# The second half of the first batch normalized on GpSimd and projected inside the first score steps, and the last projection moved ahead in the MLP

## The chip, the cores and the metric

The kernel runs on one core of a Trainium2 chip. The metric is the device time of one execution in microseconds (us). Five engines work side by side: TensorE (PE; its weight loads are shown apart as PEld), VectorE (DVE), ScalarE (ACT), GpSimd (POOL) and SyncE (SP), which issues DMAs. Each engine takes its instructions in program order and waits at semaphores for the others. TensorE writes into PSUM banks of 128 partitions x 512 float32; VectorE and ScalarE read them out.

## The reference

A block of attention and a gated MLP, with four layer norms, on x of shape (4, 1024, 256). The weights of the attention are binarized (sign times the mean magnitude of a row), those of the MLP are ternary.

```python
def attn(x, Wq, bq, Wk, bk, Wv, bv, Wp, bp):      # 16 heads of 16
    q, k, v = (split_heads(binlinear(x, W, b)) for W, b in ((Wq, bq), (Wk, bk), (Wv, bv)))
    att = softmax(einsum('bhtd,bhsd->bhts', q, k) * 16 ** -0.5)
    y = einsum('bhts,bhsd->bhtd', att, v)
    return binlinear(merge_heads(y), Wp, bp)

def ffn(x, ...):                                   # 256 -> 1024 -> 1024 -> 1024 -> 256
    h = silu(tlin(x, w1_w, w1_s)) * tlin(x, w2_w, w2_s)
    h = gelu(tlin(h, h1_w, h1_s))
    h = gelu(tlin(h, h2_w, h2_s))
    return tlin(h, w3_w, w3_s)

x = x + layernorm(attn(layernorm(x), ...))
x = x + layernorm(ffn(layernorm(x), ...))
```

## The kernel before

**Precision.** Activations that enter a product with signs or ternary weights are kept as two pieces, a rounded high part (`fp32r`) and the rest, so each product is made twice, once for each piece.

**Opening.** The tokens of the first batch come in two halves of 512. Ahead of the attention function, the first half is measured, normalized (L264), transposed (L284) and split into its two pieces (L286, L287). The second half is only measured (`measure_half(1)`). In the attention function's opening (from L1009), `norm(1, nc.vector)` normalizes the second half (L465), `first_heads(is_q, 0)` (L561) makes the queries and keys of the first four heads for the first half of the tokens: four products of 512 columns (L566), two reads of the bank by ScalarE (L572 with the scale and bias into the high part, L579 into `full`), and one VectorE instruction (L584 for queries, L587 for keys). `turn(1, k)` (L474) then transposes the second half in four products for each of two halves of the channels (L477), ScalarE copies the result (L482) and VectorE makes the rest (L485).

**Steps.** Attention is one software pipeline over steps (L1073 on); a step covers four heads. `first = -10`; a step s makes the first pass of tile s + 10 (scores of 128 queries x 512 keys for four heads, L722, each head in 32 rows of the array; VectorE takes their maxima, L731), and from s = 0 the second pass (scores again with the maximum subtracted, L768, exponentials by ScalarE, L778) and the product with the values (L794). A tile's number a tells which halves it needs: tiles 0 to 3 take first-half queries with first-half keys, tiles 4 to 7 first-half queries with second-half keys, tiles from 8 on second-half queries. When eight tiles are done, `combine` joins the maxima and `shift` (L748) turns them for the second pass.

Within a step the four heads start at slots 0, 0, 1 and 3 of five (`BEGIN`), and `run_jobs` puts side jobs at two places of the step: slot 0 behind the third of the five, slot 1 behind the last. `place((s, slot), job)` files a job. TensorE meets, in a step, three score products left over from the tile before, the slot 0 jobs, five score products of the new tile, the slot 1 jobs. The side jobs of the opening are `first_heads(.., 1)`, `value(m)` (L494, eight products of 256 columns and a copy by ScalarE), the four `part` jobs of group 0 (L535, four products of 512 columns; at steps first + 2, + 4, + 6, + 8, slot 1, written by GpSimd in L548 and L549), `alphas`, `projection_bias` (L405). Jobs of one place run in the order in which they were filed.

**Banks.** `bank()` (L305) hands out the seven PSUM banks by a planned clock; `put` and `got` state the true waits, and `got` makes each reader of a bank wait for the readers before it.

**GpSimd in the opening.** The root for the second half (L166), fills of `negmax`, of the ones in the value tiles (L436, L437), of `yn` (L441) and of `bits` (L903), two products with the identity for the value bias (L397). It is idle from 19.8 us to the copies of `part` at 35.2 us.

**MLP.** Eight blocks of 512 tokens. `hidden` (L1256) makes eight columns of 128 hidden units: for the first three columns the products of all but the last two inputs are made first, then each column is finished, passed through Gelu by ScalarE and split by VectorE (L1188, L1189), and then the jobs filed for the column in `beside` run. `norm` measures and normalizes the next block's tokens, `turn` transposes them. In block 0, `scale_y` (L1394) scales the last batch's attention output and `last_projection` (L1399) projects it (L1407), scales and shifts it (L1412, L1413), normalizes it and adds it to x. The tiles with the tag "z" have two buffers, which `norm`, `last_projection` and `down` share in turn.

Of the kernel before, what the change touches and what calls it, by code (L numbers as in the profile page):

```python
# [34 lines left out]
AF = mybir.ActivationFunctionType  # L35
ALU = mybir.AluOpType
# [10 lines left out]
def sandwich_kernel(  # L47
# [24 lines left out]
    nc = tc.nc  # L72
    B, T, C = x.shape
    F = w1T.shape[1]
    KC = C // P
# [70 lines left out]
    alpha4 = small.tile([P, 2], F32, tag="alpha4", name="alpha4", bufs=1)  # L146
    bias4 = small.tile([P, 2], F32, tag="bias4", name="bias4", bufs=1)
# [142 lines left out]
    def attention(signs):  # L290


        with ExitStack() as actx:
# [6 lines left out]
            through = ps.tile([P, 7, 512], F32, tag="through", name="through")  # L300
# [29 lines left out]
            def got(banks, engine, access, for_pe=False):  # L330

                others = [o for o in ("PE", "ACT", "DVE") if o != engine and not (for_pe and o == "PE")]
                after = [i for b in banks for i in written[b] + read[b]]
                lasts = {"ACT": 500, "DVE": 580}[engine]
                clock[engine] = max(clock["PE"] + 240, clock[engine] + lasts)
                for b in banks:
                    read[b].append(access.ins)
                    free_at[b] = clock[engine] + lasts + 150  # L340
                return state(access, engine, after, others)
# [96 lines left out]


            yn = ac.tile([P, 16, 32], F32, tag="yn", name="yn")  # L440
            nc.gpsimd.memset(yn, 1.0)  # L441

            def half_tile(name, dtype=F32):

# [116 lines left out]
            def first_heads(is_q, j):  # L561

                t = bank()
                for k in range(KC):
                    for i in range(PIECES):
                        put(t, nc.tensor.matmul(  # L566
                            through[:, t, :], sign4["q" if is_q else "k"][:, k, :],
                            xnT_of[0][i][:, k, bass.ts(j, 512)],
                            start=(k == 0 and i == 0), stop=(k == KC - 1 and i == PIECES - 1),
                        ), xnT_by[0])  # L570
                to = (q_of[0][0] if is_q else k_of[0])[:, bass.ts(j, 512)]
                got([t], "ACT", nc.scalar.activation(  # L572
                    to, through[:, t, :], AF.Identity,
                    bias=bias4[:, 0:1] if is_q else k_bias4,
                    scale=alpha4[:, 0:1] if is_q else k_alpha4,
                ))
                full = a2.tile([P, 512], F32, tag="full", name=f"full4_{is_q}_{j}")
                n = 1 - is_q
                got([t], "ACT", nc.scalar.activation(  # L579
                    full, through[:, t, :], AF.Identity, bias=bias4[:, n : n + 1],  # L580
                    scale=alpha4[:, n : n + 1],
                ))
                if is_q:
                    nc.vector.tensor_sub(q_of[0][1][:, bass.ts(j, 512)], full, to.bitcast(F32))  # L584
                else:

                    nc.vector.scalar_tensor_tensor(  # L587
                        to, full, lower, to.bitcast(F32), ALU.mult, ALU.add
                    )
# [254 lines left out]
            def place(at, job):  # L844
                jobs.setdefault(at, []).append(job)

            first = -STEPS - LEAD
# [52 lines left out]

            raw_of = {}
            bits = ac.tile([P, 512], F32, tag="bits", name="bits")
            nc.gpsimd.memset(bits, 0)  # L903

            def weight_jobs():
                loads, stay, pass_by = [], [], []
# [83 lines left out]
            def alphas(n):  # L990

                t = bank()
                if n == "v":
                    for c in range(KC):
                        for k in range(KC):
                            put(t, nc.tensor.matmul(
                                through[:, t, c : c + 1], mag_of[n][:, k, bass.ts(c, P)],
                                avg[:, 0:1], start=(k == 0), stop=(k == KC - 1),
                            ))
                    got([t], "ACT", nc.scalar.copy(alpha_sb[:, 2, :], through[:, t, :KC]))  # L1000
                else:
                    for k in range(KC):
                        put(t, nc.tensor.matmul(
                            through[:, t, :C], avg, mag_of[n][:, k, :],
                            start=(k == 0), stop=(k == KC - 1),
                        ))
                    got([t], "ACT", nc.scalar.copy(az_bc, through[:, t, :C]))

            norm, turn, value = batch_jobs(0)  # L1009
            if signs:  # L1010
                quadrants(0)
                norm(1, nc.vector)
                for is_q in (True, False):
                    first_heads(is_q, 0)
                for k in range(KC):
                    turn(1, k)

                place((first, 1), lambda: first_heads(False, 1))
                place((first + 1, 1), lambda: first_heads(True, 1))
                for i, n in enumerate("vp"):  # L1020
                    place((first + 6 + i, 0), lambda n=n: alphas(n))
                after = first + 2
            else:
                part = group_jobs(0)
                norm(0, nc.vector)
                for k in range(KC):
                    turn(0, k)
                part(True, 0, nc.vector)
                norm(1, nc.vector)
                for k in range(KC):  # L1030
                    turn(1, k)
                part(False, 0, nc.vector)
                part(False, 1, nc.vector)
                part(True, 1)
                spread(0, (nc.sync, nc.scalar))
                after = first + 3
            for m in range(NT // 2):
                place((after + m, 0), lambda m=m: value(m))
            place((first + 8, 0), projection_bias)
            place((4, 0), load_scales)  # L1040

# [70 lines left out]
    def mlp(tag, low_too, wp):  # L1114
        with ExitStack() as fctx:
# [119 lines left out]
            def norm(blk):  # L1235
                mv, rs = stats([tokens(blk, i) for i in range(4)], f"f{tag}{blk}")
                xn_of[blk] = [pair_c(f"fxn{tag}_{blk}_{i}") for i in range(2)]
                for i in range(4):
                    nc.gpsimd.tensor_scalar(
                        xn_of[blk][i // 2][:, i % 2, :], tokens(blk, i), mv[:, i, 0:1],  # L1240
                        rs[:, i : i + 1], ALU.subtract, ALU.mult,
                    )
# [156 lines left out]
            def last_projection():  # L1399

                zs = [pair_c(f"z{tag}_{i}") for i in range(2)]
                zs = [zs[i // 2][:, i % 2, :] for i in range(4)]
                for m in range(2):
                    zp = ps_o.tile([P, 512], F32, tag="o", name=f"zp{tag}_{m}")
                    for i in range(2):
                        for k in range(KC):
                            nc.tensor.matmul(  # L1407
                                zp[:, bass.ts(i, C)], yT_last[:, k, bass.ts(2 * m + i, P)],
                                wp[:, k, :].bitcast(F32), start=(k == 0), stop=(k == KC - 1),
                            )  # L1410
                        z = zs[2 * m + i]
                        nc.vector.tensor_mul(z, zp[:, bass.ts(i, C)], az_bc)  # L1412
                        nc.vector.tensor_add(z, z, bz_bc)  # L1413
                mv, rs = stats(zs, f"z{tag}")
                for i, z in enumerate(zs):
                    nc.vector.tensor_scalar(
                        z, z, mv[:, i, 0:1], rs[:, i : i + 1], ALU.subtract, ALU.mult
                    )
                    to = x_sb[:, B - 1, NT // 2 + i, :]
                    nc.gpsimd.tensor_add(to, to, z)  # L1420
# [3 lines left out]
            for blk in range(blocks):  # L1424
                h = gated(blk)
                more = blk + 1 < blocks
                beside = {2: [lambda: norm(blk + 1)]} if more else {}
                beside2 = {3: [lambda: turn(blk + 1)]} if more else {}
                if blk == 0:
                    beside[6] = [scale_y]  # L1430
                    beside2[5] = [last_projection]
                if behind:
                    measure, finish = behind
                    beside[0] = [lambda: finish(*measure())]
                g1 = hidden(blk, "g1", h1_w, h1T, sh1_sb, h, beside)
                g2 = hidden(blk, "g2", h2_w, h2T, sh2_sb, g1, beside2)
                if more:
                    nc.scalar.activation(warm2, s3_bc[:, 0:1], AF.Silu)
                behind = down(blk, g2)
# [58 lines left out]
```

## Time and profile before

| what | value |
|---|---|
| median of three runs | 1567.8 us (1567.79 to 1568.9) |
| the profiled execution's own time | 1567.72 us |
| its span, first to last instruction | 1565.9 us |
| mean granted TensorE clock | 0.993 |
| last product ahead of the attention loop (L477) | ends at 22.5 us |
| first score product (L722) | 23.30 us |
| first second-pass product (L768) | 55.48 us |
| first product of the MLP (L1218) | 904.04 us |
| length of MLP block 0; of block 1 (first gate product to first gate product) | 87.4 us; 81.2 us |

The profile is of one execution. A busy TensorE is not TensorE at its peak, since the ends of matmuls are modelled; how far apart two products start says more. In the timeline a row is a start, a duration, an engine, a line, an operation with what it writes and reads, a count of merged instructions, and in brackets the idle time ahead of it and what ended it. The granted clock is the share of the full TensorE clock that the profile's records show.

### The profile page before, as it was taken

What the parts mean: (1) busy time and instruction counts of PE and PEld (TensorE: products, weight loads), DVE (VectorE), ACT (ScalarE), POOL (GpSimd) and SP (SyncE); (2) the same over time, 40 slices, a digit from 0 to 9 for tenths busy, and PEclk for the clock granted to TensorE, in tenths of its full rate; (3) what the DMA queues carried; (4) which work ended last, traced back from release to release, by engine and by line L of the source; (5) the groups of instructions that cost most, each with busy time, mean ns of one, the idle gap of its engine ahead of it and who ended that gap; (6) DMA issues with size and microseconds to landing.
All of it is one profiled execution on the core that took longest, in us unless ns stands there. A gap on an engine that the chain in (4) does not pass through costs nothing.

```text
span 1565.9 us, 31822 instructions
## 1 busy us (share of the span) xinstructions
PE 1531.1 (98%) x12988; PEld 980.3 (63%) x12988; DVE 1075.2 (69%) x1960; ACT 829.2 (53%) x1496; POOL 437.4 (28%) x595
## 2 busy tenths in 40 slices
PE   7999999999999999999999999999999999999998
PEld 5544445444444444454444477888888888888887
DVE  6889887899787798878899554554545544455453
ACT  4577777677777677777777841413232313232321
POOL 2223143564424563314612150120202020202010
PEclk8999999999999999999999999999999999999999
DMA  1311521133132033311312040000000000000000
GB/s 58 72 30 33 144 49 29 24 72 74 39 76 59 22 65 72 66 30 31 75 36 73 8 139 0 1 14 1 14 1 14 1 14 1 14 1 14 1 14 17
DMA packets 35084, 58.55 MB, mean 37 GB/s; under 512 B 9968, under 2 KB 21488, under 8 KB 34928
## 3 DMA queue, kind: packets, MB, share of 16 engines
q1 hardware_dynamic: 29760, 43.57, 12.8%
q0 software_dynamic: 3792, 11.54, 2.3%
q8 instruction: 104, 1.70, 0.4%
q10 hardware_dynamic: 1376, 1.31, 0.2%
q14 instruction: 52, 0.43, 0.1%
HBM read 24.40 MB, written 4.19 MB: 18 GB/s over the span
## 4 chain that ended last, share of the span: by engine, by line
PE 85%; DVE 9%; ACT 4%; issue 1%; POOL 1%; DMA 1%; SPq 0%; DVEq 0%; ACTq 0%; POOLq 0%
PE g L1218 30%; PE y L794 14%; PE through L768 12%; PE through L722 10%; PE p L1218 7%; DVE nm L731 5%; PE fzp L1332 4%; PE through L535 2%; ACT e L778 2%; PE through L494 1%; PE through L748 1%; PE through L637 1%; ACT ys L809 1%; DVE bnstp_x L175 1%; DVE yt L835 1%
## 5 line engine op out<-in xcount | busy, mean ns | idle before, releaser
L731 DVE TENSOR_REDUCE nm<-through 128x1 f32<-128x512 f32 x1024 | 643.5, 680 | 115.6 <-PE through L722 59.3
L778 ACT ACTIVATE e<-through 128x512 f32<-128x512 f32 x1024 | 545.4, 603 | 160.7 <-PE through L768 141.7
L722 PE MATMUL through<-ks,qs 32*128 32x512 f32 x2048 | 462.2, 445 | 3.8 <-DVE nm L731 2.7
L768 PE MATMUL through<-qs,ks 32*128 32x512 f32 x2048 | 442.6, 434 | 11.1 <-ACT e L778 7.3
L768 PE MATMUL through<-nmT,ones_r 32*128 32x512 f32 x1024 | 348.7, 450 | 0.4 <-ACT nmT L755 0.4
L794 PE MATMUL y<-e,v 128*32 128x256 f32 x4096 | 323.0, 393 | 0.0
L722 PEld LDWEIGHTS through<-ks,qs 32*128 32x128 f32 x2048 | 215.7, 184 | 106.4 <-issue 82.5
L1218 PE MATMUL g<-g,h_sb 128*128 128x512 f32 x1024 | 235.7, 390 | 0.0
L768 PEld LDWEIGHTS through<-qs,ks 32*128 32x128 f32 x2048 | 201.8, 183 | 44.6 <-ACT e L778 20.5
L1218 PEld LDWEIGHTS g<-g,h_sb 128*128 128x128 f32 x1024 | 191.7, 188 | 39.5
L768 PEld LDWEIGHTS through<-nmT,ones_r 32*128 32x128 f32 x1024 | 137.6, 182 | 91.7 <-issue 88.7
L794 PEld LDWEIGHTS y<-e,v 128*32 128x32 f32 x4096 | 86.5, 108 | 170.8 <-issue 150.7
L1261 ACT ACTIVATE g2f<-g,sh_sb 128x512 f32<-128x512 f32 x64 | 44.1, 688 | 200.5 <-PE g L1218 180.8
L1261 ACT ACTIVATE g1f<-g,sh_sb 128x512 f32<-128x512 f32 x64 | 44.1, 689 | 170.1 <-PE g L1218 166.9
L164 POOL TENSOR_SCALAR ve_fz<-mvp_fz 128x4 f32<-128x4 f32 (+1 forms) x8 | 1.9, 232 | 468.5 <-DVE mvp_fz L176 468.5
L1218 PE MATMUL g<-h,h1b_sb 128*128 128x512 f32 x512 | 126.4, 389 | 0.0
L1218 PE MATMUL g<-h,h1a_sb 128*128 128x512 f32 x512 | 126.4, 389 | 0.0
L1188 DVE CAST g<-g2f 128x512 fp32r<-128x512 f32 x64 | 27.8, 434 | 142.0 <-ACT g2f L1261 142.0
L1218 PE MATMUL p<-xnT_sb,w_sb 128*128 128x512 f32 x512 | 117.7, 390 | 0.0
L1218 PEld LDWEIGHTS g<-h,h1a_sb 128*128 128x128 f32 x512 | 96.1, 188 | 19.9
L1218 PEld LDWEIGHTS g<-h,h1b_sb 128*128 128x128 f32 x512 | 96.1, 188 | 19.9
L1218 PEld LDWEIGHTS p<-xnT_sb,w_sb 128*128 128x128 f32 x512 | 95.6, 188 | 19.9 <-issue 0.4
(204 smaller groups left out, 1515.8 us busy)
## 6 DMA issues: line engine op xcount, KB each, us to landing
qs<-h1b_sb SPq DMA_DIRECT2D x240, 64.0 KB, 2.4
ks<-h1b_sb SPq DMA_DIRECT2D x120, 64.0 KB, 2.4
wraw<-in_dram SPq DMA_DIRECT2D x28, 256.0 KB, 2.7
h_sb<-in_dram POOLq DMA_DIRECT2D x4, 1024.0 KB, 8.5
yT<-yt SPq DMA_DIRECT2D x112, 32.0 KB, 2.0
out_dram<-x_sb SPq DMA_DIRECT2D x7, 512.0 KB, 2.8
x_sb<-in_dram SPq DMA_DIRECT2D x3, 1024.0 KB, 5.3
w_sb<-in_dram POOLq DMA_DIRECT2D x3, 1024.0 KB, 8.4
```

The costliest lines, as they stand in the source:

```text
L175: nc.vector.bn_stats(st, z)
L494: put(t, nc.tensor.matmul(through[:, t, bass.ts(i, C)], xnT_of[b][j][:, k, bass.ts(2 * m + i, P)], w_in["v"][:, k, :], start=(k == 0 and j ...
L535: put(t, nc.tensor.matmul(through[:, t, :], w_in[tag][:, k, bass.ts(c, P)], xnT_of[b][i][:, k, bass.ts(j, 512)], start=(k == 0 and i == 0) ...
L722: put(t, nc.tensor.matmul(through[:, t, :], q_of[u][n][rows, bass.ts(qt, P)], k_of[u][rows, bass.ts(j, 512)], start=(n == 0), stop=(n == 1),))
L731: got([t], "DVE", nc.vector.tensor_reduce(nm_of[blk][:, n4, j, g : g + 1], through[:, t, :], AX.X, ALU.max, negate=True))
L768: t, nc.tensor.matmul(through[:, t, :], lhs, rhs, start=(n == 0), stop=(n == 2)),
L778: exps.append(got([t], "ACT", nc.scalar.activation(e_of[s, g], through[:, t, :], AF.Exp)))
L794: nc.tensor.matmul(y_of[blk][32 * g : 32 * g + 32, cols], v_sb[n // 2][:, n % 2, :, :].rearrange("p h d -> p (h d)")[:, bass.ds((4 * g4 + ...
L1188: nc.vector.tensor_copy(hi, full)
L1218: nc.tensor.matmul(out[c], wk, src[j][:, k, :], start=(k == 0 and i == 0 and j == 0), stop=(k == n_k - 1 and i == len(ws) - 1 and j == 1),)
L1261: nc.scalar.activation(g, ps, AF.Gelu, scale=scale[:, c : c + 1])
L1332: nc.tensor.matmul(out_ps[i][:, :C], g2[j][:, k, bass.ts(i, P)], wk, start=(k == 0 and n == 0 and j == 0), stop=(k == NF - 1 and n == len( ...
```

## The change

In the opening of attention, the second half's norm goes from VectorE to GpSimd, and its two transposes leave the place ahead of the first step: they become jobs of the steps `first + 1` (slot 1) and `first + 2` (slot 0). The second half's keys and queries for the first four heads move from the steps `first` and `first + 1` to both places of `first + 3`, the values from `first + 2` on to `first + 4` on, the alphas from `first + 6` and `first + 7` (slot 0) to `first + 5` and `first + 7` (slot 1). For the first half, the second read of the bank in `first_heads` goes from ScalarE to VectorE. The fills of `yn` and `bits` go to step `first + 4`. In the MLP's block 0, `scale_y` goes from column 6 to column 0 of the first hidden layer, `last_projection` from column 5 of the second hidden layer to column 2 of the first, and the next block's norm from column 2 to column 6 of the first; in `last_projection` the eight products of a bank now all stand ahead of VectorE's reads of it.

```diff
@@ -438,7 +438,6 @@
             yn = ac.tile([P, 16, 32], F32, tag="yn", name="yn")
-            nc.gpsimd.memset(yn, 1.0)
@@ -576,10 +575,16 @@
                 full = a2.tile([P, 512], F32, tag="full", name=f"full4_{is_q}_{j}")
                 n = 1 - is_q
-                got([t], "ACT", nc.scalar.activation(
-                    full, through[:, t, :], AF.Identity, bias=bias4[:, n : n + 1],
-                    scale=alpha4[:, n : n + 1],
-                ))
+                if j == 0:
+                    got([t], "DVE", nc.vector.tensor_scalar(
+                        full, through[:, t, :], alpha4[:, n : n + 1], bias4[:, n : n + 1],
+                        ALU.mult, ALU.add,
+                    ))
+                else:
+                    got([t], "ACT", nc.scalar.activation(
+                        full, through[:, t, :], AF.Identity, bias=bias4[:, n : n + 1],
+                        scale=alpha4[:, n : n + 1],
+                    ))
@@ -900,7 +905,6 @@
             bits = ac.tile([P, 512], F32, tag="bits", name="bits")
-            nc.gpsimd.memset(bits, 0)
@@ -1009,17 +1013,17 @@
                 quadrants(0)
-                norm(1, nc.vector)
+                norm(1, nc.gpsimd)
                 for is_q in (True, False):
                     first_heads(is_q, 0)
-                for k in range(KC):
-                    turn(1, k)
-
-                place((first, 1), lambda: first_heads(False, 1))
-                place((first + 1, 1), lambda: first_heads(True, 1))
+
+                place((first + 1, 1), lambda: turn(1, 0))
+                place((first + 2, 0), lambda: turn(1, 1))
+                place((first + 3, 0), lambda: first_heads(False, 1))
+                place((first + 3, 1), lambda: first_heads(True, 1))
                 for i, n in enumerate("vp"):
-                    place((first + 6 + i, 0), lambda n=n: alphas(n))
-                after = first + 2
+                    place((first + 5 + 2 * i, 1), lambda n=n: alphas(n))
+                after = first + 4
@@ -1038,6 +1042,8 @@
             place((4, 0), load_scales)
+            place((first + 4, 0), lambda: nc.gpsimd.memset(yn, 1.0))
+            place((first + 4, 0), lambda: nc.gpsimd.memset(bits, 0))
@@ -1408,6 +1414,7 @@
                                 wp[:, k, :].bitcast(F32), start=(k == 0), stop=(k == KC - 1),
                             )
+                    for i in range(2):
                         z = zs[2 * m + i]
                         nc.vector.tensor_mul(z, zp[:, bass.ts(i, C)], az_bc)
                         nc.vector.tensor_add(z, z, bz_bc)
@@ -1427,8 +1434,7 @@
                 beside = {2: [lambda: norm(blk + 1)]} if more else {}
                 beside2 = {3: [lambda: turn(blk + 1)]} if more else {}
                 if blk == 0:
-                    beside[6] = [scale_y]
-                    beside2[5] = [last_projection]
+                    beside = {0: [scale_y], 2: [last_projection], 6: beside[2]}
```

## The prediction

> **What bounds it now.** First the page: engines and chain.
>
> ```profile
> span 1565.9 us, 31822 instructions
> PE 1531.1 (98%) x12988; PEld 980.3 (63%) x12988; DVE 1075.2 (69%) x1960; ACT 829.2 (53%) x1496; POOL 437.4 (28%) x595
> PE 85%; DVE 9%; ACT 4%; issue 1%; POOL 1%; DMA 1%; SPq 0%; DVEq 0%; ACTq 0%; POOLq 0%
> ```
>
> TensorE carries 85% of the chain, so an edit is worth what it does to TensorE's idle time and rate. Second, TensorE alone in stretches of 3.41 us (columns: stretch, its length, busy us with instructions, granted clock, DMA), and then the timeline (start, us, engine, line, operation, count, wait ahead of it).
>
> ```profile
> 16.19:19.60 3.41, 2.58 (x6) 1.00 0.00 0
> 19.60:23.01 3.41, 2.88 (x11) 1.00 0.00 0
> 23.01:26.43 3.42, 2.67 (x18) 1.00 0.01 2
> 26.43:29.84 3.41, 2.57 (x10) 1.00 0.00 0
> 29.84:33.25 3.41, 3.41 (x14) 0.50 0.02 5
> 33.25:36.66 3.41, 3.41 (x12) 0.50 0.00 0
> 36.66:40.08 3.42, 3.42 (x19) 0.50 0.00 0
> 514.53:517.94 3.41, 2.56 (x28) 1.00 0.10 14
> 517.94:521.36 3.42, 3.42 (x32) 0.50 0.17 65
> ```
>
> ```profile
> 20.57 1.91 PE L477 MATMUL through<-ident,xn 128*128 128x128 f32 x8
> 23.30 0.73 PE L722 MATMUL through<-ks,qs 32*128 32x512 f32 x5 [0.82 <-DVE ks L587]
> ...
> 32.24 0.79 PE L535 MATMUL through<-xnT_sb,w_sb 128*128 128x512 f32 x1
> 32.83 0.63 PE L535 MATMUL through<-w_sb 128*128 128x512 f32 x1
> 33.26 0.63 PE L535 MATMUL through<-xnT_sb,w_sb 128*128 128x512 f32 x1
> 34.24 1.22 PE L722 MATMUL through<-ks,qs 32*128 32x512 f32 x3
> 35.39 0.58 PE L494 MATMUL through<-w_sb,xnT_sb 128*128 128x256 f32 x1
> ```
>
> The reader is to see that the clock changes only at multiples of 3.41 us, and that a busy TensorE does not decide it: 100% busy stretches stay at 0.50. I weighted each matmul's streaming time (half clock: 0.427 us per 512 columns, the step from 32.83 to 33.26; 0.213 for 256 columns or a 128-column float32 transpose) by the share of the array that it fills (a 32-row score product a quarter) and got for the seven opening stretches 0.72, 0.78, 0.49, 0.34, 0.76, 0.67, 0.82. Half clock ends after 0.78 and 0.82, not after 0.72, 0.76 or 0.67. Full clock is lost after 0.34; likewise after 0.36 at 514.53 us; the lowest share that kept it is 0.42. Up at about 0.77, down at about 0.4 fits every change in this trace. (The first clock record is at 23.01. Ahead of it the column shows 1.00, but L566's products start 0.43 us apart there and 0.23 from 24.49 on.)
>
> Third, the timeline of the MLP's first block, where the last projection sits, and one GpSimd row.
>
> ```profile
> 970.35 1.02 PE L1407 MATMUL zp<-wp_sb,yT_last 128*128 128x256 f32 x4
> 972.86 1.99 PE L1407 MATMUL zp<-wp_sb,yT_last 128*128 128x256 f32 x8 [1.49 <-DVE z L1412]
> 975.44 1.13 PE L1407 MATMUL zp<-wp_sb,yT_last 128*128 128x256 f32 x4 [0.59 <-DVE z L1412]
> ...
> 936.28 5.06 POOL L1239 TENSOR_SCALAR fxn<-x_sb,mvp_f,rsp_f 128x256 f32<-128x256 f32 x4
> ```
>
> TensorE stands still 1.49 + 0.59 us there, waiting for VectorE's reads of the same bank.
>
> **The change part by part.** *MLP.* With all products of a bank ahead of its reads, the 2.08 us go. But the projection now stands two columns after scale_y. TensorE gets there where it now begins column 3, at 929.56. Scale_y follows column 0's split on VectorE (until 929.9) and takes 0.88 for two rows: the second operand is there at 930.85, so 1.05 us of new wait, product time taken off. Net -1.0; ends -2.1 (no wait) and 0. Behind it VectorE holds the splits of columns 3 to 5 for about 9 us, until some 946, but the second hidden layer asks for them past 950: nothing. The norm moved to column 6 ends near 959 (2.1 statistics, 1.8 root, 5.06 GpSimd), its transposes come near 967: nothing; uncovered it would cost those 5 us.
>
> *Small moves.* Two GpSimd fills (1.04 us) go to step 4, where GpSimd idles between weight copies: nothing, 1.04 uncovered. The biased copy on VectorE (0.69 as L584; rows 0.43 to 0.78) still waits for ScalarE's read of its bank; keys are ready 0.1 us earlier (0 to 0.35), at 23.2. The moved steps issue no DMA; the first DMA copies of queries and keys slide on SP with their products.
>
> *Norm on GpSimd.* Four rows of 1.23 (up to 1.66 in this trace) from 18.85, behind the last fill: done at 23.8 to 25.5. TensorE asks at 24.65 (full) or 25.5 (half clock): nothing; worst 0.85.
>
> *Transposes and second-half projections, moved.* At 20.77 TensorE ends the first four-head products and waits for the keys until 23.2; the 1.91 us of transposes, which filled that hole, come two steps later. So the stretch that lifted the clock at 23.01 falls from 0.78 to 0.34 (1.17 us of products). The next ones hold score products and half-rate transposes: I count 0.64 and 0.50. From step 2 to 7 every step now carries two jobs, each 0.16 us of start-up gap and each followed by a score group that fills 1.15 us with 0.3 to 0.5 of array time: at best 0.74 in any stretch. The 0.82 that lifted the clock at 40.08 came from a step with one job, whose eight score products ran unbroken (37.40); the new order has such a step only at its start. So half clock until the second passes.
>
> Cost from 23.2 to the first second pass (55.48 now): 18 score groups, ten 512-column or value jobs, two transposes, the alphas, the projection bias, the shift. At half clock: 18 x 1.15 (34.24 to 35.39) + 10 x 2.0 (32.24 to 34.24) + 2 x 1.0 + 1.8 + 2 x 1.9 + 1.05 = 49.35, ending at 72.55: +17.1. At full clock (0.66 and 1.13, from 41.04 to 42.84 in the timeline; value 1.15, the rest 4.8 together) 28.1 plus 1.8 of waits for banks that VectorE holds, ending at 53.1: -2.4. Those are the ends; I take half clock, which the counted shares support. The clock then rises in the first second passes; one more stretch at half clock costs at most 1.7 (half of 3.41), I take 0.8 (0 to 5.1, three stretches).
>
> A rule speaks against this reading. The Trainium skill, "TensorE: Matmul & The Clock Gate", Part 4, says that transposes do not count as busy for the clock, and Part 1 that it falls after an idle window of about 3.4 us. Here it fell after a stretch with 0.84 us idle, and rose after one that was mostly transposes. By the page the transposes' absence costs no clock, and the sum would be the full-clock one below, 1564.3, not 1584.6.
>
> *Sum.* 1567.72 (this execution's own time, span 1565.9 plus 1.8 around it; the median of the runs is 1567.8) + 17.1 + 0.8 - 1.0 = 1584.6. Its own range: 1580 to 1589.
>
> **The rivals.** *A, clock back midway.* My best stretches are within 0.03 of the 0.77 that lifts it. Lifted at 43.5, in step 4: a half-done job and 3.5 us a step after it put the last first pass at 55.2 instead of 50.35: +4.85 - 1.0 = 1571.6; between 1568.5 and 1580 by the stretch.
>
> *B, faster: full clock throughout.* The early products run 17.0 to 20.8 without a hole, so in about half the positions of the 3.41 us grid one stretch passes 0.77 and lifts the clock near 20 to 21. If it then held, VectorE's maxima would run nearly unbroken from 24: -2.4 - 1.0, 1564.3. Against: the next stretch has under 0.8 us of array time, 0.24. It decides if the share that keeps full clock is in truth below that.
>
> *C, no gain, no loss.* Clock lifted near 33: the opening ends where it does now, and the -1.0 is below what can be told: 1567.
>
> **How the numbers follow.** 0.2% (3.1 us) is about what a measurement of this kernel can tell. Forecast 0.46, A 0.25, B 0.17, C 0.12. Of A four fifths lie above 1570.9: slower 0.46 + 0.20 = 0.66; B gives faster 0.17; C and the rest of A, same 0.17. The time is the forecast's, 1584.6. The range reaches down through A and C to 1565 and up to 1588, leaving out most of B and the forecast's top.
>
> **What would show it.** Granted clock 0.50 from the opening's first records to past 60 us; score groups 1.15 us apart from jobs of 2.0; the transposes in step 1 to 2 behind GpSimd's four rows; TensorE idle 20.8 to 23.2; L768 first at about 72; L1407 in one piece near 947 with one wait, for scale_y. Wrong: the clock column at 1.00 through 30 to 45 us, L768 before 55.5, or a GpSimd norm past 26 on which a transpose waits.

## The result, and the profile after

The changed kernel takes 1584.05 us (median of four runs, 1582.94 to 1585.72), the kernel before 1567.8 beside it (four runs, 1563.4 to 1568.9). The ratio is 1.0125, 95% interval 1.0102 to 1.0148: it is slower. The profiled execution took 1584.12 us, span 1582.3.

The page of the changed kernel, engines and chain:

```profile
span 1582.3 us, 31820 instructions
PE 1547.3 (98%) x12988; PEld 990.9 (63%) x12988; DVE 1073.3 (68%) x1958; ACT 828.0 (52%) x1494; POOL 442.6 (28%) x599
PE 85%; DVE 9%; ACT 3%; issue 1%; POOL 1%; DMA 0%; SPq 0%; DVEq 0%; ACTq 0%; POOLq 0%
```

The same number of products is 16.2 us busier on TensorE (1547.3 against 1531.1), and its weight loads 10.6; GpSimd has 5.2 us more to do, VectorE and ScalarE 1.9 and 1.2 less. So the products themselves ran slower somewhere. The timeline of TensorE and GpSimd in the changed kernel (start, us, engine, line, operation, count, wait ahead of it) shows where:

```profile
20.08 0.63 PE L565 MATMUL through<-w_sb 128*128 128x512 f32 x1
23.28 2.07 PE L727 MATMUL through<-ks,qs 32*128 32x512 f32 x13 [2.56 <-DVE ks L592]
25.36 1.08 PE L476 MATMUL through<-ident,xn 128*128 128x128 f32 x4
...
30.65 0.80 PE L534 MATMUL through<-xnT_sb,w_sb 128*128 128x512 f32 x1 [0.86 <-DVE w_sb L484]
...
43.27 0.80 PE L534 MATMUL through<-xnT_sb,w_sb 128*128 128x512 f32 x1
43.86 0.63 PE L534 MATMUL through<-w_sb 128*128 128x512 f32 x1
44.29 0.63 PE L534 MATMUL through<-xnT_sb,w_sb 128*128 128x512 f32 x1
...
73.51 0.64 PE L773 MATMUL through<-qs,ks 32*128 32x512 f32 x3
```

The reader is to see the empty hole from 20.7 to 23.28 us, and at 43.86 two products 0.43 us apart, where the kernel before had the same two 0.24 apart, in its timeline:

```profile
41.38 0.40 PE L535 MATMUL through<-w_sb 128*128 128x512 f32 x1
41.62 0.40 PE L535 MATMUL through<-xnT_sb,w_sb 128*128 128x512 f32 x1
```

The first second-pass product comes at 73.51, 18.03 us later than before (55.48). The chain of waits of the changed kernel (start, us, engine, line, count) is all TensorE from 30.61 us on, with the two durations that the prediction had summed; a part of it:

```profile
33.88 2.00 PE through L565 x4
35.88 1.15 PE through L727 x4
37.03 2.00 PE through L565 x4
39.03 1.15 PE through L727 x3
40.18 2.01 PE through L493 x8
```

In the stretches of TensorE alone (stretch, length, busy us with instructions, granted clock, DMA) the column misleads: the first clock record of this execution is at 80.82 us, and ahead of a first record the column says 1.00, whatever the clock was. The same 3.41 us hold 27 instructions ahead of it and 51 behind it.

```profile
77.41:80.82 3.41, 3.41 (x27) 1.00 0.57 101
80.82:84.23 3.41, 3.41 (x51) 1.00 0.61 106
```

In the MLP the last projection is one piece with one wait, as the timeline of the changed kernel shows:

```profile
948.22 3.72 PE L1413 MATMUL zp<-wp_sb,yT_last 128*128 128x256 f32 x16 [0.96 <-DVE yT_last L1400]
```

| stretch, read from the timelines | before, us | after, us | difference |
|---|---|---|---|
| start to the first second-pass product | 55.48 | 73.51 | +18.03 |
| from there to the first MLP product | 848.56 | 848.07 | -0.5 |
| MLP block 0 | 87.32 | 85.97 | -1.35 |
| the rest | 574.57 | 574.78 | +0.2 |

MLP block 0 of the kernel before is 87.32 us by its timeline, not 87.4. The second row of the table holds two things: the clock came up only 7.3 us into the second passes, and the profile before has two half-clock stretches in the attention (from 517.95 and 736.4 us), the one after only one (from 319.75).

### The profile page after: what moved, and what is told of

The parts are those of the page before. It is cut to its first block, busy times and chain, and to the rows that moved or that the text cites. A ratio compares the mean times of both kernels' runs of the same rounds, so it can differ in the third digit from the quotient of the medians.

```text
span 1582.3 us, 31820 instructions
## 1 busy us (share of the span) xinstructions
PE 1547.3 (98%) x12988; PEld 990.9 (63%) x12988; DVE 1073.3 (68%) x1958; ACT 828.0 (52%) x1494; POOL 442.6 (28%) x599
## 4 chain that ended last, share of the span: by engine, by line
PE 85%; DVE 9%; ACT 3%; issue 1%; POOL 1%; DMA 0%; SPq 0%; DVEq 0%; ACTq 0%; POOLq 0%
PE g L1224 29%; PE y L799 14%; PE through L773 12%; PE through L727 10%; PE p L1224 7%; DVE nm L736 5%; PE fzp L1338 4%; PE through L534 3%; ACT e L783 2%; PE through L493 1%; PE through L753 1%; PE through L642 1%; ACT ys L814 1%; DVE bnstp_x L175 1%; DVE yt L840 1%
## 5 line engine op out<-in xcount | busy, mean ns | idle before, releaser
L727 PE MATMUL through<-ks,qs 32*128 32x512 f32 x2048 | 470.7, 455 | 4.6 <-DVE ks L592 2.6
L727 PEld LDWEIGHTS through<-ks,qs 32*128 32x128 f32 x2048 | 220.4, 188 | 109.8 <-issue 85.9
```

The costliest lines, as they stand in the source:

```text
L727: put(t, nc.tensor.matmul(through[:, t, :], q_of[u][n][rows, bass.ts(qt, P)], k_of[u][rows, bass.ts(j, 512)], start=(n == 0), stop=(n == 1),))
```

## The experiments

The theory: TensorE ran at half clock from 17 to 80.8 us, because the transposes no longer fill the hole behind the first products, and because steps with two jobs each never use the array densely enough to lift the clock again. The rivals: GpSimd's slower norm is late; the new order itself makes TensorE wait; the MLP part costs something.

### The moved jobs alone

To the kernel before, only these moves; norm, second read, fills and MLP stay:

```diff
-                for k in range(KC):
-                    turn(1, k)
-                place((first, 1), lambda: first_heads(False, 1))
-                place((first + 1, 1), lambda: first_heads(True, 1))
+                place((first + 1, 1), lambda: turn(1, 0))
+                place((first + 2, 0), lambda: turn(1, 1))
+                place((first + 3, 0), lambda: first_heads(False, 1))
+                place((first + 3, 1), lambda: first_heads(True, 1))
                 for i, n in enumerate("vp"):
-                    place((first + 6 + i, 0), lambda n=n: alphas(n))
-                after = first + 2
+                    place((first + 5 + 2 * i, 1), lambda n=n: alphas(n))
+                after = first + 4
```

> The kernel before, with only the second half's transposes, its keys and queries, the values and the alphas moved to their new steps; the norm stays on VectorE, the second read of the bank on ScalarE, the fills and the MLP as before. Theory (the granted clock: the hole behind the first products is left empty and every step then has two jobs): half clock to past 70 us, first second-pass product at 71 to 74 us, time 1583 to 1587, that is the whole loss and without the MLP's gain of about 1.3. Rival (GpSimd's slower norm, or the second read on VectorE, is what costs): those are not in this kernel, so within 3 us of the kernel before.

Measured 1585.49 us (1585.07 to 1586.04), ratio 1.0130 (1.0102 to 1.0158); first second-pass product at 73.58 us, first clock record at 83.23. The moved jobs carry the whole loss. GpSimd's norm and VectorE's second read, which this kernel lacks, are worth nothing (73.58 against 73.51).

### The transposes back in the hole

The changed kernel with `norm(1, nc.vector)` and

```diff
+                for k in range(KC):
+                    turn(1, k)
-                place((first + 1, 1), lambda: turn(1, 0))
-                place((first + 2, 0), lambda: turn(1, 1))
```

> The changed kernel, with the norm back on VectorE and the two transposes back ahead of the first step; all the other moves stay. It tells the two parts of the theory apart. If the empty hole alone keeps the clock down: clock up near 23 us and kept, time 1564 to 1569. If a second part is needed (low array use in steps 0 to 2 drops the clock near 27 to 30 us, and steps with two jobs each never lift it again): clock up near 23, down by 30, then half to past 65 us, time 1577 to 1583. Rival (GpSimd's norm is late): 1564 to 1568, with the clock no different from the changed kernel.

Measured 1581.09 us (1580.63 to 1582.46), ratio 1.0105 (1.0076 to 1.0133); first second-pass product at 70.45. TensorE by stretches of 3.41 us, on this execution's own grid (the clock changes only at the ends of such stretches, and where they lie differs between executions; stretches from 29.02 to 76.81 are left out):

```profile
18.79:22.20 3.41, 3.41 (x13) 1.00 0.00 0
22.20:25.61 3.41, 2.50 (x18) 1.00 0.01 2
25.61:29.02 3.41, 3.41 (x9) 0.50 0.00 0
76.81:80.22 3.41, 3.41 (x32) 0.50 0.57 101
80.22:83.63 3.41, 3.41 (x48) 1.00 0.62 106
```

The clock records begin at 22.20, at full, fall to 0.50 after one stretch and stay there up to 80.22. So with the hole filled the clock does rise, and it is not enough: the first steps lose it, and the two-job steps that follow don't bring it back. Of the 18 us the filled hole returns 3.06, and that is about what the transposes took in their new place, 2 x 1.0 us and the wait of 0.86. The larger part of the theory, the steps, is shown; that the hole has to be empty for the loss is not.

### Products added, nothing taken away

The changed kernel with products whose results nobody reads, five in the hole and four in each of steps 0, 1 and 2 (the function is shortened here to the kind that this kernel uses):

```diff
+                def fill(n):
+                    b = bank()
+                    for _ in range(n):
+                        put(b, nc.tensor.matmul(
+                            through[:, b, :], sign4["q"][:, 0, :],
+                            xnT_of[0][0][:, 0, 0:512], start=True, stop=True,
+                        ), xnT_by[0])
+                    free_at[b] = clock["PE"]
+                fill(5)
+                place((first, 1), lambda: fill(4))
+                place((first + 1, 0), lambda: fill(4))
+                place((first + 2, 0), lambda: fill(4))
```

> The changed kernel with 17 products more, whose results nobody reads: five of 512 columns in the hole at 20.8 us and four in each of steps 0, 1 and 2. Nothing is taken away and the order of the rest stays. Theory (clock): up by 21 to 24 us and kept, first second-pass product at 53 to 57 us, time 1562 to 1568. Rival (the new order itself makes TensorE wait, or there is more work on the path): the products only add 17 x 0.43 at half clock, so 1584 to 1591.

Measured 1576.16 us, ratio 1.0071 (1.0043 to 1.0099); four runs at 1569.38, 1575.94, 1576.38 and 1576.41. The profile is of the first: full clock from 19.87 to 60.83, first second-pass product at 56.52, 17 us earlier for 17 products more. More work made the kernel faster, which the rivals don't allow. In this profile the clock rose behind the first products alone (the stretch from 16.46 to 19.87); what the fillers did is keep it. But the time lies above the range that was expected; three of the four runs are 7 us longer than the profiled one, which is itself 1.4 us above that range.

### The same fillers, thin

Each filler fills 32 columns of the array instead of 128 (`through[0:32, b, :]`, `sign4["q"][:, 0, 0:32]`), for the same time.

> As the kernel with 17 products more, but each fills only 32 of the 128 columns of the array, for the same time. Theory (the share of the array decides, not that TensorE is busy): the clock stays down as in the changed kernel, time 1583 to 1590. Rival (any busy TensorE lifts the clock): as with the full products, 1562 to 1568.

Measured 1575.69 us (ten runs, 1566.21 to 1577.4), ratio 1.0048 (1.0026 to 1.0069). The theory lost this one: products with a quarter of the columns lift the clock like full ones. The profile, at 1576.43 us (first second-pass product at 64.58), shows the clock kept at 25.35 behind a stretch that thin fillers helped to fill, and also what the longer runs suffer (stretches in between are left out):

```profile
21.94:25.35 3.41, 2.73 (x14) 1.00 0.00 0
...
39.00:42.42 3.42, 3.42 (x23) 1.00 0.00 0
42.42:45.84 3.42, 3.42 (x27) 1.00 0.22 38
45.84:49.25 3.41, 3.41 (x11) 0.50 0.00 0
69.72:73.14 3.42, 3.42 (x30) 0.50 0.57 101
73.14:76.55 3.41, 3.41 (x52) 1.00 0.62 109
```

The clock falls behind the stretch from 42.42 to 45.84, which holds the eight one-column products of the alphas (0.98 us from 42.98): TensorE is 100% busy in it and its array has next to nothing to do for more than a quarter of it. It comes back only at 73.14.

### Thin the other way

The same count and places, but 32 rows and all columns (`sign4["q"][0:32, 0, :]`, `xnT_of[0][0][0:32, 0, 0:512]`), into a bank of its own.

> As the kernel with thin fillers (17 products of 512 columns in the hole and in steps 0, 1 and 2), but thin the other way: each product uses 32 of the 128 rows and all columns, into a bank of its own. Theory, mended after the thin fillers lifted the clock (rows in use count, columns don't): clock down as in the changed kernel, up only past 65 us, time 1583 to 1590. Rival (any busy TensorE lifts the clock): up by 24 us, first second-pass product at 55 to 66, time 1566 to 1578.

Measured 1588.13 us (1586.76 to 1589.83), ratio 1.0151 (1.0109 to 1.0194); first second-pass product at 75.87.

```profile
17.99:21.40 3.41, 3.41 (x9) 1.00 0.00 0
21.40:24.82 3.42, 2.53 (x18) 1.00 0.00 0
24.82:28.23 3.41, 3.41 (x14) 0.50 0.00 0
...
50.00:60.00 10.00, 10.00 (x38) 0.50 0.08 13
```

Here the grid lay so that one stretch (17.99 to 21.40) was filled by the first products, which end near 20.7, and the first fillers; the clock came up for one stretch, fell again and stayed at half until 86.26. Fillers with few rows don't hold it, fillers with few columns do. So in these two shapes it is the rows in use that count, and neither the columns nor that TensorE is busy. (The two kernels differ in the fillers' bank too, which no run here varies by itself.) The kernel is 4 us slower than the changed one; as an estimate, its 17 products at 0.43 us each at half clock come to 7.3 us, of which the five in the hole end ahead of the first score product and cost nothing.

### Transposes as fillers

Ten float32 transposes of 128 x 128 in the hole and eight in each of steps 0, 1 and 2.

> The changed kernel with transposes as fillers: ten of 128 x 128 float32 in the hole and eight in each of steps 0, 1 and 2, the same streaming time as the full products. Theory (transposes count for the clock like products): up by 24 us, first second-pass product at 55 to 66 us, 1567 to 1578. Rival (transposes do not count): half clock to past 65 us, 1583 to 1592.

Measured 1576.16 us (seven runs, 1568.77 to 1577.44), ratio 1.0071 (1.0044 to 1.0098), the time of the full products. In the profile the clock is at full from 20.27 to 44.16, falls there, again at the alphas, and is back at 74.89; first second-pass product at 64.48. Four of its stretches:

```profile
16.86:20.27 3.41, 3.34 (x8) 1.00 0.00 0
20.27:23.68 3.41, 1.93 (x16) 1.00 0.00 0
40.75:44.16 3.41, 3.41 (x26) 1.00 0.21 35
44.16:47.58 3.42, 3.42 (x15) 0.50 0.02 4
```

The first products alone lifted the clock at 20.27. The transposes kept it over the hole, where the kernel of the next experiment, without fillers there, loses it. Transposes count for the clock. The Trainium skill, "TensorE: Matmul & The Clock Gate", Part 4, says that they do not count as busy in the same way; here they held the clock as the products did, and the measurement decides.

### One dense run of products

The changed kernel with eight full products behind the second half's keys, and no others (`place((first + 3, 0), lambda: fill(8))`).

> The changed kernel with one run of eight products more behind the second half's keys in step 3, 3.4 us long at half clock. Theory (two jobs a step cannot lift the clock by themselves, a stretch without gaps does, and then the steps keep it): clock up at 39 to 43 us, kept or lost once at the alphas, first second-pass product at 60 to 68, time 1570 to 1580. Rival (the clock would need the early steps to be full): half to past 75 us and 1586 to 1589.

Measured 1575.8 us (four runs: 1570.85, 1571.39, 1580.22, 1583.3), ratio 1.0081 (1.0049 to 1.0114). The profile is at 1571.39 us (stretches from 27.03 to 33.85 are left out):

```profile
16.79:20.20 3.41, 3.33 (x8) 1.00 0.00 0
20.20:23.61 3.41, 0.84 (x9) 1.00 0.00 0
23.61:27.03 3.42, 3.42 (x17) 0.50 0.01 2
33.85:37.27 3.42, 3.42 (x10) 0.50 0.02 5
37.27:40.68 3.41, 3.41 (x18) 1.00 0.00 0
```

Again the early products lifted the clock for one stretch (20.20 to 23.61), and the stretch with the hole in it, 0.84 us busy, lost it. The dense run brought it up at 37.27, and the two-job steps then kept it: first second-pass product at 59.27, both a little earlier than expected. So an empty hole does not keep the clock down for good; what the new order lacks is one dense stretch behind it. The runs at 1580.22 and 1583.3 have no profile. Their mean granted clocks, 0.985 and 0.987 against 0.992 and 0.994 in the two shorter runs, say that they were longer at half clock; whether from the alphas on stays open.

### Full clock all through the new order

The changed kernel with fillers in the hole (five), steps 0 and 1 (four each), behind the second transposes in step 2 (three), and four beside the alphas in step 5; here `fill` takes no third argument to `put`, so that the fillers wait for nothing.

> The changed kernel with fillers in the hole and in steps 0, 1 and 2 (the last now behind the second transposes, three products), and four more beside the alphas in step 5, where the profile of the kernel with thin fillers shows the clock fall at 45.8 us. Theory (the one-column products of the alphas use so little of the array that a stretch around them can drop the clock): full clock from 22 us to the second passes in nearly all runs, first second-pass product at 54 to 57 us, 1563 to 1569, without the group of runs at 1576. Rival (the runs at 1576 have another cause, later in the kernel): two groups as before, near 1569 and 1576.

Measured 1565.99 us (eleven runs, 1564.53 to 1568.89), ratio 1.0008 (0.9996 to 1.0021). There is no group at 1576. That fits the alphas as its cause: both profiles of that group, of the kernels with thin fillers and with transposes, lose the clock there, and the mean granted clock is 0.988 to 0.991 in the seven long runs with thin fillers, 0.997 or 0.998 in their three short ones, and 0.995 to 0.999 in the eleven runs here. (The fillers of step 2 and what they wait for changed as well, so the alphas were not varied alone.) First second-pass product at 56.27, with the clock at full from 22.88 to the last products:

```profile
39.95:43.36 3.41, 3.41 (x23) 1.00 0.11 19
43.36:46.77 3.41, 3.41 (x23) 1.00 0.11 19
46.77:50.19 3.42, 3.42 (x21) 1.00 0.00 0
```

With the clock given back, the first second pass is within 0.8 us of the kernel before, and the time is the same: the clock is the whole of the loss, as far as these times can tell. A gain of the new order doesn't show, with 20 added products in the kernel.

### The MLP part alone

The kernel before with `beside = {0: [scale_y], 2: [last_projection], 6: beside[2]}` and the split loop in `last_projection`.

> The kernel before with the MLP part of the change alone. Theory: MLP block 0 (first gate product to first gate product) 86.1 us instead of 87.4, one wait of about 1 us ahead of the last projection instead of two of 1.49 and 0.59; the time 1.3 below the kernel before, less than the spread of its runs (1561 to 1569), so it is read from the trace. Rival (VectorE's backlog of 9 us or the later norm makes the second hidden layer wait): block 0 87.4 or longer.

Measured 1564.03 us (ten runs, 1558.67 to 1565.93), ratio 0.9990 (0.9974 to 1.0006): no difference that the times can show. The timeline of this kernel has the gain:

```profile
925.60 3.72 PE L1407 MATMUL zp<-wp_sb,yT_last 128*128 128x256 f32 x16 [0.68 <-DVE yT_last L1394]
```

MLP block 0 takes 85.64 us, 1.68 less than before. The same profile shows how the opening can vary with no change to it: with the very opening of the kernel before, its clock was up at 21.41, down at 24.82 and up at 28.24, one half-clock stretch instead of three, and the first second pass began at 51.28 instead of 55.48. (It lost the clock once more, for two stretches from 55.55, in the second passes.)

### The old order with the clock held

The kernel before with the MLP part, two fillers ahead of the second half's keys in step 0 and four behind its queries in step 1.

> The kernel before with the MLP part of the change and six products more whose results nobody reads: two of 512 columns in step 0 and four in step 1, where TensorE waits (24.0 and 27.9 us). Theory (clock): the stretch near 26 to 30 us stays above the share that drops the clock, so full clock from 23 us on, first second-pass product near 52, MLP block 0 86.1 us long; 1558 to 1563 in most runs, 3 to 6 below the kernel before. Rival (the half-clock stretch of the kernel before costs nothing, since VectorE's maxima bind there): 1564 to 1567.

Measured 1561.47 us (twelve runs, 1559.9 to 1568.61), ratio 0.9982 (0.9969 to 0.9995). TensorE at the place where the kernel before lost the clock, first by stretches, then rows of the timeline:

```profile
22.09:25.50 3.41, 2.48 (x13) 1.00 0.01 2
25.50:28.92 3.42, 2.15 (x14) 1.00 0.00 0
28.92:32.33 3.41, 3.41 (x20) 1.00 0.02 5
```

```profile
23.93 0.73 PE L1020 MATMUL through<-xnT_sb,w_sb 128*128 128x512 f32 x2
24.50 0.47 PE L566 MATMUL through<-xnT_sb,w_sb 128*128 128x512 f32 x1
...
28.73 1.20 PE L1020 MATMUL through<-xnT_sb,w_sb 128*128 128x512 f32 x4 [1.27 <-DVE nm L731]
29.86 0.73 PE L722 MATMUL through<-ks,qs 32*128 32x512 f32 x3
```

Full clock from 22.09 on, first second-pass product at 52.19, 3.3 us ahead of the kernel before in its profile and 4.1 ahead of the new order at full clock, which has 20 fillers instead of six. The first two fillers fill a wait: the next product starts at 24.50, as in the kernel before (24.49). The other four don't: they stand behind a wait of 1.27 us that VectorE's maxima (L731) end, and the score products behind them come at 29.86 instead of 28.76. This kernel has the lowest median of all, 0.18% below the kernel before. How much of that is the fillers' is not shown, since the MLP part alone gives a ratio of 0.9990 and its ten runs (1558.67 to 1565.93) overlap with the twelve here.

## Why the prediction was right

**Time and direction.** 1584.6 forecast, 1584.05 measured; the mechanism named as likeliest, half clock up to the second passes, is the one that the runs show. That the sum comes within 0.6 us is partly luck: the opening is 0.96 us longer than in it, the second passes come out 1.3 shorter, the MLP 0.35 shorter, the rest 0.2 longer.

**Opening.** The price of 18 score groups at 1.15 and ten jobs at 2.0 gave a first second pass at 72.55 us; it came at 73.51. Most of the difference is a wait that was not in the sum: the first group's queries (L534 at 30.65) stand 0.86 us for the rest of the second transposes (L484), although they read only the first half's columns. Up to there the chain of waits runs over VectorE, whose maxima take 4.87 us of it, and not over TensorE's jobs as the sum had it.

**The clock.** The forecast that no stretch would pass what lifts it held in every run of the changed kernel and of the moved jobs alone (1582.94 to 1586.04 together). Of its two parts, the two-job steps carry the loss: with the hole filled again the kernel still takes 1581.09 us, and with an empty hole one dense run brings the clock back. The hole's own part is at most the 3.06 us that the filled hole returned. What was off is the weight: array area was counted, with a quarter for few rows and a quarter for few columns, and the thin fillers show that columns don't count. In the opening the two counts are the same, since nothing there is thin in columns but the alphas, so the sum was not touched. One reading doesn't come out again: the same count gives the stretch from 29.84 about 0.72, not 0.76; the other six agree. The bounds are also less sharp than 0.77 and 0.4: by the same count the changed kernel's clock came up behind a stretch of 0.72 (from 77.41), after one of 0.73 (from 53.51) had not lifted it, and a stretch of 0.36 (from 44.10 with the one dense run) kept full clock where one of 0.37 (from 42.42 with thin fillers) lost it. So the margin that kept the clock down, 0.03 by the prediction's own words, was thin; it held in the eight runs there are. The sign in the profile was half wrong: the forecast looked for 0.50 in the clock column through the opening, and the column says 1.00 up to the first record; the spacing of the products shows it instead.

**Second passes.** Predicted +0.8 for one more slow stretch; the profile has the clock down for 7.3 us of them, up to 80.82, and the first product with the values comes 7.5 us after the first second pass instead of 6.3, so +1.2 there. One half-clock stretch fewer later in the attention (one against two; at most 1.7 us, half of 3.41) more than pays for it, and the row ends at -0.5. That last part is luck: no part of the forecast speaks of it.

**MLP.** Predicted -1.0 with a new wait of 1.05 for scale_y; measured -1.35 with a wait of 0.96, and -1.68 with 0.68 by itself. The backlog on VectorE and the later norm cost nothing that shows, as forecast: the block got shorter by more than the sum said.

**GpSimd's norm.** Predicted done at 23.8 to 25.5 us and hidden. One row of the changed kernel's timeline:

```profile
18.78 5.54 POOL L464 TENSOR_SCALAR xn<-x_sb,mvp_x,rsp_x 128x256 f32<-128x256 f32 x4
```

It ends at 24.32, TensorE asks at 25.36.

**The rivals.** Full clock throughout was priced at 1564.3, with the opening done at 53.1; with the clock held by fillers it was done at 56.27. Of the 15 fillers behind the hole 12 stand in its chain of waits, 3 x 1.13 us, which as an estimate leaves 52.9; the 53.1 itself was not tried without them. That early products can lift the clock for one stretch, and that the next stretch loses it, happened as written, in the kernels with one dense run and with few-row fillers.

## What to carry to other kernels

Ahead of moving TensorE work out of a wait, ask what the clock makes of the wait: count, in stretches of the length at which the trace shows the clock change, the streaming time of products that use all rows, and compare it with the stretches ahead of which the clock rose and fell. Count the steps behind the wait as well as the wait: here the transposes, put back into the hole, returned 3.06 us of 18, and eight products more in one step 14.2 (59.27 against 73.51). Where real work can't make a stretch dense, products that nobody reads can, but they cost their own time wherever they don't end ahead of the work that the wait is for: 3 x 1.13 us in the kernel with full clock.

## What was not expected

- Few-column products (128 rows x 32 columns) hold the clock at full, few-row products (32 x 128) don't: 1575.69 against 1588.13 us with the same 17 products.
- A TensorE that the profile shows 100% busy can lose its clock: behind eight one-column products of 0.98 us within one stretch, and then stay at half for 27 us.
- The position of the 3.41 us grid differs between executions (first change at 23.01 in one profile, 21.41 in another with the same opening); the first second pass came 4.2 us earlier in the second. The kernel before spreads from 1560.78 to 1568.71 us in 29 runs (median 1564.56), and its mean granted clock goes with the time: 0.997 or 0.998 in the five shortest runs (up to 1561.54), 0.991 in the five longest (from 1568.3). So most of that spread is time at half clock. That the grid's position sets it was seen in two profiles only.
